# A graph network with a hand-drawn engine order: longer planned landing times for layer 0's turns and loads, the last h added up by VectorE and GpSimd, and x loaded ahead of adj

## The chip, the core and the metric

The kernel runs on one core of one Trainium2 chip. A core has five engines that take instructions in order, each from its own queue: TensorE (PE, matrix products into PSUM), VectorE (DVE), ScalarE (ACT), GpSimd (POOL) and SyncE (SP, which here issues nearly all DMAs). PEld in the profile is PE's loading of weights. Engines wait for each other through semaphores. The metric is the device time of one execution in microseconds (us); lower is better.

## What is computed

The input x is 32 batches of 512 nodes with 128 features; adj is one 512 x 512 matrix.

```python
# layer 0: seven terms; both adjacencies are adj
y = x W0 + (adj x)(W1 + W4) + (adj^2 x)(W2 + W5) + (adj^3 x)(W3 + W6)
h = layernorm(x + y)
h0 = h
for _ in range(5):                      # layer 1: gated steps
    m = adj h                           # in_matrix and out_matrix are both adj
    u = h u3.T + ub3
    z = sigmoid([m, m] w3.T + b3 + u)
    r = sigmoid([m, m] w4.T + b4 + u)
    hv = tanh([m, m] w5.T + b5 + (r h) u5.T + ub5)
    h = (1 - z) h + z hv
out = layernorm(h0 + h)
```

Everything is fp32.

## The kernel before

Batches go in 16 pairs (q = 0 to 15, b = 0 and 1). Each pair goes through layer 0 (`layer0`, L692), then five steps (`pair`, L1022, s = 0 to 4). Products of two batches are done by Strassen's scheme with seven block products instead of eight (`seven`, L384), whose sums of operands are made by POOL (`add`, L501) and whose results are taken from PSUM by ACT copies (L376) and VectorE additions (L380). From pair 2 on, two pairs share one quarter-block product with adj (`quad_product`, L556). PE computes the transposed adj, adj^2 and the sums of their blocks (T at L228, TT at L243) once at the start.

**What sets the order.** The kernel first describes every operation to a planner (`Plan`, L47): its engine, a cost in us, what it comes after, which buffers it takes and gives back, a key, and `late`, the time between the end of its cost and the moment at which its result counts as there. Then `run` (L75) plays the engines through: whenever an engine is free, it takes the ready operation with the lowest key whose buffers are free, and emits it. That order, fixed before the launch, is the order in each engine's queue. The chip keeps to it: an instruction that waits holds up all that stand behind it in its queue. `KEYS` (L24) gives each pair its base key, `TT_KEY` and `SQ_KEY` those of the start's sums and of the square of adj. The slots (L157) are the buffers; `two` and `inside` are counters without a tile, which limit how many block products and pairs are open at once in the plan.

**Turns.** Between a step and the next, h has to be transposed. `turn` (L336) does it without PE: VectorE transposes 32 x 32 blocks (L351), SP writes them to memory by four DMAs (L343, cost 1.76, late 1.8), and one more DMA fetches them (L349, cost 0.35, late 2.8). In layer 0, `turn_nodes` (L356) uses it for x and for h0 and ends with an ACT copy (L361) from the fetched raw tile (a `v` slot, five of them) into xT or hT. Only pairs 14 and 15 in their last two steps use PE's transpose instead (L1090 and L1093, `ON_PE`).

**The end of the last two pairs.** `gates` (L890) makes z, r and hv. In an ordinary step POOL adds (1-z)h and z hv at L954. In the last step of pairs 14 and 15 (`quick`) it hands two parts over: h becomes (1-z)h (VectorE, L945 for pair 14, L933 for pair 15) and z becomes z hv (L947, L927). PE then adds three things in PSUM by products with the identity: h0, the transposed h part and the transposed z part (`finish`, L994, matmuls at L1002; `last_finish`, L957, matmuls at L968, where everything is done in halves). `norm` (L295) takes statistics on VectorE (L304, L305), raises to -1/2 on POOL (L308 to L313) and applies on ACT (L321) or, for the very last batch, on VectorE (L317).

**The start.** SP issues in the order of the keys: first half of the first x, two quarters of adj, second half of x, two more quarters of adj (L208), the second x (L198, its first half), w0 (L251), the gate weights (L271, L279), then the rest of x. The second x is `x_in[1]` at L220.

Of the kernel before, what the change touches and what calls it, by code (L numbers as in the profile page):

```python
# [15 lines left out]
NK = 4  # L16
# [6 lines left out]
ON_PE = {14: 2, 15: 2}  # L23
KEYS = [-2.0, 20.0, 50.0, 68.0, 88.0, 124.0, 154.0, 168.0, 186.0, 214.0, 234.0, 272.0, 298.0, 330.0, 346.0, 362.0]  # L24
LONG = 19.0
TT_KEY = 39.0
SQ_KEY = 16.0
KEPT = 3
# [98 lines left out]
def gnn_resnorm_kernel(  # L127
# [26 lines left out]
    def tiles(tag, n, shape=(P, N), pool=work):  # L154
# [20 lines left out]
        v=tiles("v", 5),  # L175
        two=[None] * 4,
        inside=[None] * 16,
    )
# [17 lines left out]

    def load_x(q, b):
        nc.sync.dma_start(plan[f"xg{q}"][:, b], x[2 * q + b].rearrange("(p k) c -> p k c", k=NK))  # L198

    def loaded_x(q, key, late=2.9):  # L200

        take = [("xg", f"xg{q}")]
        first = plan("SP", 0.42, lambda: load_x(q, 0), take=take, key=key, late=late)
        return first, plan("SP", 0.42, lambda: load_x(q, 1), after=[first], key=key, late=late)

# [5 lines left out]
    def first_x():  # L211
        emit = lambda: load_x(0, 0)
        a = plan("SP", 0.42, emit, take=[("xg", "xg0")], key=-99.0, late=2.9)
        b = plan("SP", 0.42, lambda: load_x(0, 1), key=-91.0, late=4.0)
        return a, b
# [3 lines left out]
    at_in = [in11, in21, load_adj(0, 1, -90.0), load_adj(1, 1, -90.0)]  # L219
    x_in[1] = loaded_x(1, -80.0, 5.5)  # L220

# [41 lines left out]
    w0_ready = plan("DVE", 2.3, layer0_weights, after=[w0_in], give=[("UY", "w0")], key=-40.0)  # L263


    ready = []

    def gate_weight(src, name):
        halves = lambda: plan[name][:, : 2 * P].rearrange("p (h o) -> p h o", h=2)
        w = const.tile([P, P], F32, tag=name, name=name)  # L270
        emit = lambda: nc.sync.dma_start(halves(), src.rearrange("(h c) o -> c h o", c=P))  # L271
        got = plan("SP", 0.45, emit, take=[("z", name)], key=23.0, late=6.5)
        emit = lambda: nc.vector.tensor_tensor(w, halves()[:, 0, :], halves()[:, 1, :], ALU.add)
        ready.append(plan("DVE", 0.28, emit, after=[got], give=[("z", name)], key=26.0))
        return w

    def plain(src, name):
        t = const.tile(list(src.shape), F32, tag=name, name=name)
        ready.append(plan("SP", 0.45, lambda: nc.sync.dma_start(t, src), key=23.5, late=4.0))  # L279
        return t  # L280
# [54 lines left out]

    def turn(src_of, dst_of, name, after, key, take=(), give=()):  # L336

        def put():
            for g in range(NR):
                nc.sync.dma_start(  # L343
                    plan[f"d{name}"][:, :, g, :].rearrange("r l f -> l r f"),
                    plan[f"v{name}"][g * R : (g + 1) * R, :].rearrange("l (r f) -> l r f", r=NR),
                )

        def fetch():
            nc.sync.dma_start(dst_of(), plan[f"d{name}"].rearrange("r l g f -> (r l) (g f)"))  # L349

        blocks = lambda: nc.vector.transpose(plan[f"v{name}"], src_of())  # L351
        t = plan("DVE", 0.7, blocks, after=after, take=[("v", f"v{name}")], give=give, key=key)
        t = plan("SP", 1.76, put, after=[t], take=[("d", f"d{name}")], give=[("v", f"v{name}")], key=key, late=1.8)
        return plan("SP", 0.35, fetch, after=[t], give=[("d", f"d{name}")], take=take, key=key, late=2.8)

    def turn_nodes(src_of, dst, name, after, key):  # L356

        raw = f"w{name}"
        src = lambda: src_of().rearrange("p k (s d) -> p s k d", d=R)
        t = turn(src, lambda: plan[raw], name, after, key, take=[("v", raw)])  # L360
        emit = lambda: nc.scalar.copy(  # L361
            plan[dst].rearrange("p (k r l) -> p k r l", k=NK, r=NR),
            plan[raw].rearrange("p (r k l) -> p k r l", k=NK, r=NR),
        )
        return plan("ACT", 0.6, emit, after=[t], give=[("v", raw)], key=key)
# [326 lines left out]
    def layer0(q, key, entered):  # L692
# [23 lines left out]
        def t_block(b, g):  # L716
            if not quad:
                return plan[f"t{q}_{b}"][:, g * HN : (g + 1) * HN]
            return plan[Mn][:, 2 * g + (q - SINGLE) % 2, b * HN : (b + 1) * HN]

        x_turned = []
        for b in range(2):
# [166 lines left out]

    def gates(name, m, h, after, u_done, quick, key, ends_here=False):  # L890

# [26 lines left out]
        if ends_here:  # L918

            new = []  # L920
            for g in range(2):
                c = slice(g * HN, (g + 1) * HN)
                emit = lambda c=c: mm(ph, u5s, rh, False, True, c)
                p4 = plan("PE", 0.43, emit, after=[p3, r], key=key + 0.3 + 0.1 * g)
                emit = lambda c=c: nc.scalar.activation(plan[ph][:, c], plan[ph][:, c], AF.Tanh, bias=hv_b)
                t = plan("ACT", 0.43, emit, after=[p4], key=key + 0.3 + 0.1 * g)
                emit = lambda c=c: nc.vector.tensor_tensor(plan[z][:, c], plan[ph][:, c], plan[z][:, c], ALU.mult)  # L927
                new.append(plan("DVE", 0.42, emit, after=[t, zs], key=key + 0.3 + 0.1 * g))
            plan("-", 0.0, lambda: None, after=new, give=[("bank", ph), ("rh", rh)], key=key)
            rest = f"rest{name}"  # L930
            emit = lambda: nc.scalar.activation(plan[rest], plan[pz], AF.Sigmoid, scale=-1.0)
            k = plan("ACT", 0.59, emit, after=[pre_z, zs], take=[("uT", rest)], give=[("bank", pz)], key=key + 0.2)
            emit = lambda: nc.vector.tensor_tensor(plan[h], plan[rest], plan[h], ALU.mult)  # L933
            k = plan("DVE", 0.69, emit, after=[k, r], give=[("uT", rest)], key=key + 0.2)
            return [k, k], new
        emit = lambda: mm(ph, u5s, rh, False, True)
# [3 lines left out]
        if quick:  # L940
# [6 lines left out]
            emit = lambda: nc.vector.tensor_tensor(plan[z], plan[ph], plan[z], ALU.mult)  # L947
            return k, plan("DVE", 0.69, emit, after=[t, zs], give=[("bank", ph)], key=key + 0.8)

# [7 lines left out]
    def last_finish(q, b, name, h, parts, h0_of, after, key, done):  # L957

        z = f"z{name}"
        keep, new = parts  # L960
        banks = [f"bt{name}{g}" for g in range(2)]
        over = []
        for g in range(2):
# [14 lines left out]
            t = plan("PE", 0.22, emit, after=list(after), take=[("bank", banks[g])], key=key + 0.6)  # L978
            emit = lambda summed=summed: summed(lambda k: plan[h][:, chunk(k)], True, False, False)
            t = plan("PE", 0.22, emit, after=[t, keep[g]], key=key + 0.1)  # L980
            emit = lambda summed=summed: summed(lambda k: plan[z][:, chunk(k)], True, False, True)
            over.append([plan("PE", 0.22, emit, after=[t, new[g]], key=key)])
        y = lambda k: plan[banks[k // H]][:, chunk(k % H)]
        give = [("bank", bank) for bank in banks] + [("hT", h), ("z", z)]
        normed = norm(NK, f"1_{2 * q + b}", y, lambda k: h0_of(b)[:, k, :], over, give, key + 0.2, b == 1)
# [8 lines left out]
    def finish(q, b, name, h, parts, h0_of, after, key, done):  # L994

        bn, z = f"bt{name}", f"z{name}"
        y = lambda k: plan[bn][:, chunk(k)]
# [12 lines left out]

        keep, new = parts
        emit = lambda: summed(lambda k: h0_of(b)[:, k, :], False, True, False)
        t = plan("PE", 0.44, emit, after=list(after), take=[("bank", bn)], key=key)
        emit = lambda: summed(lambda k: plan[h][:, chunk(k)], True, False, False)
        t = plan("PE", 0.44, emit, after=[t, keep], give=[("hT", h)], key=key)
        emit = lambda: summed(lambda k: plan[z][:, chunk(k)], True, False, True)
        t = plan("PE", 0.44, emit, after=[t, new], give=[("z", z)], key=key)
        over = norm(NK, f"1_{2 * q + b}", y, lambda k: h0_of(b)[:, k, :], [t], [("bank", bn)], key + 10, q == NP - 1 and b == 1)
# [3 lines left out]
    def pair(q, key0):  # L1022
# [6 lines left out]
        for s in range(STEPS):  # L1029
# [23 lines left out]
            if last and q < NP - KEPT:  # L1053
                emit = lambda: nc.sync.dma_start(plan[f"h0{q}"], plan[f"hd{q}"])
                take, give = [("h0", f"h0{q}")], [("hd", f"hd{q}")]
                fetched = plan("SP", 0.45, emit, after=[spilt] + got[0], take=take, give=give, key=key + 5, late=3.0)
            if s > 0:
# [11 lines left out]
            for b in range(2):  # L1069
# [3 lines left out]
                ends_here = quick and q == NP - 1  # L1073
                d = gates(nm, f"m{nm}", h[b], got[b], u_done[b], quick, key + 10 + 0.05 * b, ends_here)
                if ends_here:
                    last_finish(q, b, nm, h[b], d, h0_of, read[b], key + 10.3 + 0.05 * b, done)
                    h_done.append(d[0] + d[1])
                    continue
                if quick:
                    finish(q, b, nm, h[b], d, h0_of, read[b], key + 15, done)  # L1080
                    h_done.append(list(d))
                    continue
# [90 lines left out]
```

## Time and profile before

| what | value |
|---|---|
| median of 3 runs (lowest, highest) | 1514.92 us (1513.14, 1515.15) |
| the profiled execution: time, span | 1513.85 us, 1512.1 us |
| mean granted TensorE clock | 0.998 |
| busy share PE, VectorE, POOL, ACT | 99%, 68%, 56%, 50% |
| DMA queue, share of 16 engines | 33.6% |
| first matmul, last matmul's end | 3.62 us, 1503.46 us |

The page and its views are read so. A row of a timeline has start, duration, engine, line, operation, output<-input, shape and count, and in brackets the idle time before it and what ended it. `xN` counts records; a fp32 matmul is two records, and a transpose by PE one. SPq is SP's issuing of a DMA; its landing is another time. A matmul's end is modelled, so short waits of PE show better in the distance of starts than in idle time. A row of waits has the engine and line that waited, the one waited for, us in total, times, and the longest.

The shapes that matter: PE's products of one step and one batch are five of 128x512 (L1036, L898), 0.859 us each, and its share of seven block products, each two matmuls of 128x256 (L515, 0.864 us for the two). An addition of 128x512 takes 682 ns on VectorE (L952) and 1272 ns on POOL (L954). The DMAs land, median from the issue, after 1.8 us (d<-v), 2.8 us (X<-d and v<-d), 3.0 us (x), 4.7 us (adj) and 3.8 us (hd<-h, the 512 KB spill of h0).

### The profile page before, as it was taken

Reading aid. Unit: us, or ns where it says so; the run is one execution under the profiler, and the core shown is the slowest. Engines: PE = TensorE matmul, PEld = TensorE weight load, DVE = VectorE, ACT = ScalarE, POOL = GpSimd, SP = SyncE. Lnnn points to the kernel's source line nnn. Section 1 sums busy time; section 2 is a strip of 40 time slices with the busy share of each in tenths; the row PEclk is TensorE's granted clock in tenths of the full one; section 3 lists DMA queues with packets and bytes.
Section 4 is the critical chain, followed back from the end, with each engine's and each line's share of the span. In section 5 each row is a group of like instructions: output and inputs, shape, how many; then the busy total and the mean of one; then the engine's idle time right before and its main releaser. Section 6 shows DMA issues by size and latency. Waiting matters only on the chain.

```text
span 1512.1 us, 21105 instructions
## 1 busy us (share of the span) xinstructions
PE 1494.5 (99%) x6594; PEld 1045.6 (69%) x6594; DVE 1025.3 (68%) x2125; ACT 750.3 (50%) x1584; POOL 839.5 (56%) x1201
## 2 busy tenths in 40 slices
PE   8999999999999999999999999999999999999997
PEld 7877767666666767676776766676776776566665
DVE  6567676577766676767677576777577675766565
ACT  3354444553644554555455454645445545545454
POOL 4755835573644864766367454557654653544442
PEclk9999999999999999999999999999999999999999
DMA  3224423253233433343343243433542322432210
GB/s 96 71 56 112 113 70 105 70 146 91 79 103 92 138 106 104 96 121 94 88 124 86 77 128 103 119 91 83 148 123 60 90 71 79 118 97 77 74 46 35
DMA packets 166176, 142.91 MB, mean 95 GB/s; under 512 B 18992, under 2 KB 128048, under 8 KB 166064
## 3 DMA queue, kind: packets, MB, share of 16 engines
q1 hardware_dynamic: 166064, 141.57, 33.6%
q8 instruction: 52, 0.85, 0.2%
q14 instruction: 60, 0.49, 0.1%
HBM read 71.76 MB, written 69.73 MB: 94 GB/s over the span
## 4 chain that ended last, share of the span: by engine, by line
PE 93%; DMA 3%; SPq 2%; DVE 1%; issue 0%; ACT 0%; POOL 0%; POOLq 0%; DVEq 0%; ACTq 0%
PE bank L898 35%; PE bank L515 31%; PE bank L1036 9%; PE bank L755 6%; PE bank L820 5%; PE bank L619 5%; SPq L343 1%; DMA v<-d 1%; DMA d<-v 1%; PE bank L451 1%; DVE v L351 0%; PE bank L293 0%; DMA X<-d 0%; PE bank L1002 0%; DMA xg<-in_x 0%
## 5 line engine op out<-in xcount | busy, mean ns | idle before, releaser
L954 POOL TENSOR_TENSOR hT<-z,hT 128x512 f32<-128x512 f32 x156 | 197.8, 1272 | 286.0 <-DVE z L952 268.1
L515 PE MATMUL bank<-T,S 128*128 128x256 f32 x1232 | 307.9, 380 | 2.9 <-ACT m L376 2.4
L515 PEld LDWEIGHTS bank<-T,S 128*128 128x128 f32 x1232 | 229.0, 190 | 81.5 <-ACT m L376 34.8
L376 ACT COPY m<-bank 128x256 f32<-128x256 f32 x320 | 119.0, 372 | 274.3 <-PE bank L515 272.8
L515 PE MATMUL bank<-at,S 128*128 128x256 f32 x824 | 211.4, 380 | 0.1
L380 DVE TENSOR_TENSOR m<-bank,m 128x256 f32<-128x256 f32 x240 | 100.6, 419 | 141.2 <-PE bank L515 90.1
L515 PEld LDWEIGHTS bank<-at,S 128*128 128x128 f32 x824 | 153.1, 190 | 56.7 <-issue 35.3
L950 DVE TENSOR_TENSOR bank<-bank,hT 128x512 f32<-128x512 f32 x156 | 108.2, 695 | 108.5 <-ACT bank L938 107.4
L898 PE MATMUL bank<-m,w4s 128*128 128x512 f32 x320 | 159.5, 593 | 0.0
L1036 PE MATMUL bank<-hT,u3s 128*128 128x512 f32 x320 | 159.3, 593 | 0.0
L898 PE MATMUL bank<-rh,u5s 128*128 128x512 f32 (+1 forms) x324 | 159.1, 587 | 0.0
L898 PE MATMUL bank<-m,w3s 128*128 128x512 f32 x320 | 156.8, 593 | 0.0
L898 PE MATMUL bank<-m,w5s 128*128 128x512 f32 x320 | 155.4, 593 | 0.0
L906 ACT ACTIVATE bank<-bank 128x512 f32<-128x512 f32 x160 | 93.3, 583 | 116.0 <-DVE bank L904 115.4
L904 DVE SCALAR_TENSOR_TENSOR bank<-bank,b4s,uT 128x512 f32<-128x512 f32 x160 | 119.8, 751 | 44.3 <-PE bank L898 42.2
L1041 ACT ACTIVATE uT<-bank,ub3s 128x512 f32<-128x512 f32 x160 | 109.6, 686 | 80.8 <-PE bank L1036 79.4
L938 ACT ACTIVATE bank<-bank,hv_b 128x512 f32<-128x512 f32 x158 | 104.3, 662 | 75.5 <-PE bank L898 73.8
L911 DVE SCALAR_TENSOR_TENSOR bank<-bank,b3s,uT 128x512 f32<-128x512 f32 x160 | 119.1, 751 | 11.1 <-PE bank L898 9.6
L913 ACT ACTIVATE z<-bank 128x512 f32<-128x512 f32 x160 | 95.0, 595 | 59.3 <-DVE bank L911 53.6
L351 DVE STREAM_TRANSPOSE v<-hT 128x512 f32<-128x512 f32 x152 | 105.8, 700 | 20.7 <-POOL hT L954 17.8
L907 DVE TENSOR_TENSOR rh<-bank,hT 128x512 f32<-128x512 f32 x160 | 108.0, 680 | 6.8 <-ACT bank L906 5.7
L952 DVE TENSOR_TENSOR z<-bank,z 128x512 f32<-128x512 f32 x156 | 105.5, 682 | 1.8
(183 smaller groups left out, 2447.5 us busy)
## 6 DMA issues: line engine op xcount, KB each, us to landing
d<-v SPq DMA_DIRECT2D x832, 64.0 KB, 1.8
X<-d SPq DMA_DIRECT2D x152, 256.0 KB, 2.8
v<-d SPq DMA_DIRECT2D x56, 256.0 KB, 2.8
xg<-in_x SPq DMA_DIRECT2D x32, 256.0 KB, 3.0
out<-h SPq DMA_DIRECT2D x30, 256.0 KB, 2.1
hd<-h SPq DMA_DIRECT2D x13, 512.0 KB, 3.8
h<-hd SPq DMA_DIRECT2D x13, 512.0 KB, 3.9
at<-in_adjT SPq DMA_DIRECT2D x4, 256.0 KB, 4.7
```

The costliest lines, as they stand in the source:

```text
L351: blocks = lambda: nc.vector.transpose(plan[f"v{name}"], src_of())
L376: return "ACT", COPY[cols], lambda src: nc.scalar.copy(dst(i, j), src)
L515: nc.tensor.matmul(dst, lhsT=left[:, k, :], rhs=right[:, k, :], start=(first and k == 0), stop=(last and k == H - 1), skip_group_check=True,)
L898: nc.tensor.matmul(plan[dst][:, c], lhsT=w, rhs=plan[src][:, c], start=first, stop=last, skip_group_check=True)
L904: emit = lambda: nc.vector.scalar_tensor_tensor(plan[pr], plan[pr], b4s, plan[uT], ALU.add, ALU.add)
L907: emit = lambda: nc.vector.tensor_tensor(plan[rh], plan[pr], plan[h], ALU.mult)
L911: emit = lambda: nc.vector.scalar_tensor_tensor(plan[pz], plan[pz], b3s, plan[uT], ALU.add, ALU.add)
L950: emit = lambda: nc.vector.tensor_tensor(plan[ph], plan[ph], plan[h], ALU.subtract)
L952: emit = lambda: nc.vector.tensor_tensor(plan[z], plan[ph], plan[z], ALU.mult)
L954: emit = lambda: nc.gpsimd.tensor_tensor(plan[h], plan[z], plan[h], ALU.add)
L1036: emit = lambda bn=bn, hb=h[b]: nc.tensor.matmul(plan[bn], lhsT=u3s, rhs=plan[hb], start=True, stop=True)
L1041: emit = lambda bn=bn, uT=uT: nc.scalar.activation(plan[uT], plan[bn], AF.Identity, bias=ub3s)
```

## The change

Planner constants: four base keys move later or earlier by up to 8, the sums TT come later, the square earlier, and five block products may be open instead of four. The plan's landing times: 5.0 instead of 2.8 for the fetch of a `turn_nodes`, 5.0 instead of 3.0 for the fetch of spilled h0, 4.5 instead of 2.9 for x, 5.0 instead of 6.5 for the three gate weights, which (with the other small weights) moreover may not start before 26 us of the plan. The first x's second half goes ahead of adj in SP's queue. The second x is issued by ACT once the first block of pair 0's first product is there. In `gates` the last step adds z hv to h: on POOL for pair 14 and for batch 1 of pair 15, on VectorE in halves for batch 0 of pair 15; pair 15's (1-z)h goes from VectorE to POOL. The two finishes lose their third sum.

```diff
-KEYS = [-2.0, 20.0, 50.0, 68.0, 88.0, 124.0, 154.0, 168.0, 186.0, 214.0, 234.0, 272.0, 298.0, 330.0, 346.0, 362.0]
+KEYS = [-2.0, 20.0, 50.0, 68.0, 92.0, 118.0, 154.0, 168.0, 186.0, 214.0, 234.0, 268.0, 294.0, 322.0, 346.0, 358.0]
-TT_KEY = 39.0
-SQ_KEY = 16.0
+TT_KEY = 45.0
+SQ_KEY = 10.0
...
-        two=[None] * 4,
-        inside=[None] * 16,
+        two=[None] * 5,
+        inside=[None] * 17,
...
-    def loaded_x(q, key, late=2.9):
+    def loaded_x(q, key):
...
+        first = plan("SP", 0.42, lambda: load_x(q, 0), take=take, key=key, late=4.5)
+        return first, plan("SP", 0.42, lambda: load_x(q, 1), after=[first], key=key, late=4.5)
+
+    def second_x(after):
+
+        emit = lambda b: load_x(1, b, nc.scalar)
+        after = after + [place]
+        first = plan("ACT", 0.45, lambda: emit(0), after=after, key=-60.0, late=3.2)
+        return first, plan("ACT", 0.45, lambda: emit(1), after=after, key=-60.0, late=3.2)
...
-        b = plan("SP", 0.42, lambda: load_x(0, 1), key=-91.0, late=4.0)
+        b = plan("SP", 0.42, lambda: load_x(0, 1), key=-98.0, late=3.4)
...
-    x_in[1] = loaded_x(1, -80.0, 5.5)
...
+    place = plan("-", 0.0, lambda: None, take=[("xg", "xg1")], key=-99.0)
+    later = plan("-", 0.0, lambda: None, key=-99.0, late=26.0)
...
-        got = plan("SP", 0.45, emit, take=[("z", name)], key=23.0, late=6.5)
+        got = plan("SP", 0.45, emit, after=[later], take=[("z", name)], key=23.0, late=5.0)
...
-        t = turn(src, lambda: plan[raw], name, after, key, take=[("v", raw)])
+        t = turn(src, lambda: plan[raw], name, after, key, take=[("v", raw)], late=5.0)
...
+        if q == 0:
+            x_in[1] = second_x([got[0][0]])
...
-            emit = lambda: nc.vector.tensor_tensor(plan[h], plan[rest], plan[h], ALU.mult)
-            k = plan("DVE", 0.69, emit, after=[k, r], give=[("uT", rest)], key=key + 0.2)
-            return [k, k], new
+            emit = lambda: nc.gpsimd.tensor_tensor(plan[h], plan[rest], plan[h], ALU.mult)
+            k = plan("POOL", 1.27, emit, after=[k, r], give=[("uT", rest)], key=key + 0.2)
+            over = []
+            for g, c in enumerate(cols):
+                engine, us, by = ("POOL", 0.73, nc.gpsimd) if ends_here == 2 else ("DVE", 0.42, nc.vector)
+                emit = lambda c=c, by=by: by.tensor_tensor(plan[h][:, c], plan[h][:, c], plan[z][:, c], ALU.add)
+                over.append(plan(engine, us, emit, after=[new[g], k], key=key + 0.3 + 0.1 * g))
...
-            return k, plan("DVE", 0.69, emit, after=[t, zs], give=[("bank", ph)], key=key + 0.8)
+            t = plan("DVE", 0.69, emit, after=[t, zs], give=[("bank", ph)], key=key + 0.8)
+            emit = lambda: nc.gpsimd.tensor_tensor(plan[h], plan[h], plan[z], ALU.add)
+            return plan("POOL", 1.27, emit, after=[t, k], give=[("z", z)], key=key + 0.8)
...
-            emit = lambda summed=summed: summed(lambda k: plan[h][:, chunk(k)], True, False, False)
-            t = plan("PE", 0.22, emit, after=[t, keep[g]], key=key + 0.1)
-            emit = lambda summed=summed: summed(lambda k: plan[z][:, chunk(k)], True, False, True)
-            over.append([plan("PE", 0.22, emit, after=[t, new[g]], key=key)])
+            emit = lambda summed=summed: summed(lambda k: plan[h][:, chunk(k)], True, False, True)
+            over.append([plan("PE", 0.22, emit, after=[t, parts[g]], key=key)])
...
-        t = plan("PE", 0.44, emit, after=[t, keep], give=[("hT", h)], key=key)
-        emit = lambda: summed(lambda k: plan[z][:, chunk(k)], True, False, True)
-        t = plan("PE", 0.44, emit, after=[t, new], give=[("z", z)], key=key)
+        t = plan("PE", 0.44, emit, after=[t, parts], give=[("hT", h)], key=key)
...
-                fetched = plan("SP", 0.45, emit, after=[spilt] + got[0], take=take, give=give, key=key + 5, late=3.0)
+                fetched = plan("SP", 0.45, emit, after=[spilt] + got[0], take=take, give=give, key=key + 5, late=5.0)
```

Since the order is drawn up anew from these numbers, nearly every row of every engine's queue stands elsewhere in the changed program; PE's operations are the same but for the 16 sums of z.

## The prediction

> **What bounds the kernel now.** I read the page first, for the busiest engine, then PE's waits, then ACT's waits, then the timeline round the longest PE wait, and last the timeline of the tail.
>
> ```profile
> PE 1494.5 (99%) x6594; PEld 1045.6 (69%) x6594; DVE 1025.3 (68%) x2125; ACT 750.3 (50%) x1584; POOL 839.5 (56%) x1201
> ...
> PE 93%; DMA 3%; SPq 2%; DVE 1%; issue 0%; ACT 0%; POOL 0%; POOLq 0%; DVEq 0%; ACTq 0%
> ```
>
> PE has 99% of the span, and the chain that ended last is 93% PE. Time can leave only as PE work, as PE waits, or at the two ends. PE's own waits are few (us in total, times, longest):
>
> ```profile
> PE bank L293 <- DMA xg<-in_x: 4.2, 2, 3.6
> PE bank L515 <- ACT m L376: 2.4, 2, 1.7
> PE bank L755 <- ACT UY L376: 1.1, 1, 1.1
> PE bank L515 <- ACT uT L376: 0.5, 1, 0.5
> PE bank L293 <- ACT h L321: 0.4, 1, 0.4
> PE bank L619 <- DVE M L377: 0.2, 1, 0.2
> ```
>
> Since the modelled end of a matmul hides short waits, I also took PE's start-to-start times against the cadence of undisturbed rows (two 256-column matmuls 0.864 us, one of 512 columns 0.859, one of 128 columns 0.223, a transpose 0.11). The excess: 2.3 us by 7.7 us (x and adj landing), 0.6 at 38.1, 2.5 from 51.0 to 56.2, and 4.1 after that: 0.3 at 65, 0.6 at 138, 1.86 at 187.5, 0.88 at 249.8, 0.16 at 216, 0.35 at 985.6. Some 9.5 us, with nothing between 986 and the tail. Before them lie 3.62 us to the first matmul, behind them a tail of 8.6 us from PE's end (1503.46) to 1512.1.
>
> ACT's waits say what lies behind the largest:
>
> ```profile
> ACT xT L361 <- DMA v<-d: 22.8, 17, 5.2
> ACT hT L361 <- DMA v<-d: 8.6, 9, 1.9
> ```
>
> L361 is the copy that ends a turn of layer 0's tiles through memory. The timeline of the longest wait, its lines picked out:
>
> ```profile
> 179.41 0.45 SPq L1049 DMA_DIRECT2D hd<-h  x1
> ...
> 179.90 0.43 SPq L349 DMA_DIRECT2D v<-d  x1
> ...
> 186.42 0.62 ACT L361 COPY xT<-v 128x512 f32<-128x512 f32 x1 [5.21 <-DMA v<-d]
> ...
> 186.94 0.36 ACT L376 COPY m<-bank 128x256 f32<-128x256 f32 x1
> ...
> 187.45 1.10 PE L515 MATMUL bank<-T,S 128*128 128x256 f32 x4 [1.69 <-ACT m L376]
> ```
>
> The fetch, issued just after a 512 KB store, took 6.5 us; the plan allows 2.8. ACT runs in order, so the copy at L376, whose bank was full, sat behind L361 and PE behind it. The waits at 249.8 (L361 idle 1.63 us) and 51.0 (L361 idle 2.17 us) have the same shape.
>
> **Part 1, the sum of h moved off PE.** For pairs 14 and 15, 16 matmuls by the identity (sums of z) go. L1002's groups of four start 0.89 us apart: 16 x 0.223 = 3.57 us of PE work. Pair 14's eight (1.79 us) are on the path. In their place pair 14 gets two POOL adds of 1.27 us (L954's row). By the built order some 6 us of PE rows stand between its last u5s product and the sums that need the adds; the way there is 0.2 + 0.66 (tanh) + 0.69 + 1.27 + hand-overs = 3.2 us, so it is covered; without the cover each batch would show 1.3 us.
>
> For pair 15 I count from the first w4s product (1491.22 is zero): last sum at +12.24, last statistic +14.5, end +20.88. The changed order has four h0 sums less behind zero (0.89 us, moved ahead of it) and eight z sums less, and PE would be done at +9.55 if nothing made it wait. But the built program makes the second u5s half of each bank wait for the tanh of its first half, and each z product wait for both halves. ACT has z of batch 1, a norm row and the 1-z sigmoid after all four tanhs. Step by step, rows of before: first u5s half ends +5.58, tanhs +5.78 to +6.67, second halves end +6.8 and +7.25, z product +7.0 to +7.43, its tanhs +7.5 to +8.4, then ACT 0.6 + 0.45 + 0.6 to +10.05, POOL's (1-z)h 1.27 to +11.4, two half adds of 0.73 (L502's row of that size) to +12.9, transposing sums to +13.45, two statistics to +14.5. That is the old +14.5, hence no more than 0.1 us for the end. What stays is that zero itself comes 1.79 - 0.89 = 0.89 us earlier. **Tail: -1.0 us** (bounds -2.0 and +0.8, by what ACT and POOL find in front).
>
> A rule speaks against this part. GPSIMD Engine Reference, 4.1, sends elementwise work to VectorE, GpSimd being about twice as slow with two inputs. The trace has L954 at 1272 ns and VectorE's same-size add (L952) at 682. By the rule batch 1's three steps on VectorE would take 0.69 + 0.42 + 0.42 = 1.53 us for POOL's 2.73, and the tail -2.2; the change keeps them on POOL, so the row's sum stands.
>
> **Part 2, longer landing times.** A fetch of a turn_nodes goes from 2.8 to 5.0 us in the plan, so ACT's order has 2.2 us more of other work ahead of each such copy. Of the 26 waits at L361 all but one (5.21) are 2.2 or less. The one would keep 3.0, and PE had 3.5 us of cover there (5.21 - 1.69). So 1.86 + 0.88 go: -2.74. The other 1.35 us after 57 us have other causes and I keep them; the new keys also redraw everything, and in the new order one quarter product follows its producer directly, +0.2 to +0.5. The raw tiles are held longer, out of five v slots; DVE's waits for one (L351 on d<-v) are 2.3 us in all, off PE's path. **After 57 us: -2.4** (bounds -3.9 and +1).
>
> **Part 3, the start.** Both halves of the first x go ahead of adj. The six loads are the same, and T's first sum waits for adj until 7.75 in before; a transfer behind that one doesn't come earlier. PE does its first four groups by about 7.1 instead of 8.57 but then waits for T. What is gained is DVE's time: T's sums took 1.23, 0.88 and 1.21 us beside POOL's sums of x, and 0.68 alone. SBUF — State Buffer, the section on the shared port pair ("The single rule"), says a VectorE instruction with two SBUF inputs and a GpSimd one that reads SBUF block each other. With x at about 4.4, POOL's sums are done before T's start: some 0.5 us by the first T product. With the rule unheeded the start would give 0; I take -0.5 (0 to -1.5). The second x moves from SP, where its second half was issued behind ten weight loads at 11.60, to ACT, two issues of 0.33 to 0.59 us (SP's rows) about 8.3; the next thing in ACT's queue, a copy of transposed adj, is due only about 10. It costs nothing; uncovered it would be 1.2. POOL's sums of it start near 12.0 instead of 14.5, which helps layer 0's sums behind them. At 38.1 one transpose now stands between producer and user: -0.3. At 51.0 the copy stands two ACT rows later: 1.3 + 0.5 go, but the normalised h0 that PE needs at 56.2 hangs on statistics, POOL's two powers (ready 53.6) and four ACT rows of 0.5, about 55.3: -0.9. The weights now go out on SP behind pair 2's x and the first turn's four writes (about 30 to 34 us); with 6.0 us, the longest row of such a load, they land by 38, and VectorE asks for them about 37.5. Below nothing they can't be, since they were early before; above, 1 us. I take +0.2. **Start: -1.5** (bounds -3.5 and +1).
>
> The slots "two" and "inside" are counters of the plan without a tile, the later spill fetch is only a plan time: nothing beyond the order.
>
> **Sum.** -1.0 - 2.4 - 1.5 = -4.9. The profiled execution took 1513.85 us (span 1512.1 and 1.75 around it): 1508.95. It lies 1.07 below the median of the runs, 1514.92; carried to the median, 1510.0. What is late next: PE itself, with 1485.7 us of work.
>
> **Rivals.** (a) The forecast, 1510.0; chance 0.60. (b) Most of what hides in waits goes: L361's and the others' too, and the start passes on its 1.5 us: -1.5 - 3.8 - 2.5 = -7.8, 1507.1. For it: from 986 us on before shows no wait at all. Against: the start's chain of norms. 0.18. (c) The redrawn order opens as many waits as it closes, and the change does not do what its landing times say: tail -1.0, start -0.9, nothing else: -1.9, 1513.0. For it: 6.5 us is longer than the 5.0 planned, and h and x turns share SP with all others, where SP waited 77 us for writes to land. 0.17. (d) Slower, by the turn of h between steps when only pairs 13 to 15 are left: PE rows between the last u5s of one step and the next product exceed the way over VectorE, POOL, SP and two landings by only 2.6 us at the closest place, near 1390. Each turn that takes over 2.6 us more than its rows costs the rest at once. To end slower it would have to lose 4.9 + 3 us, three turns at 5 us over. Against: the old order has the same 2.6 us there and no wait. 1518.5, chance 0.05.
>
> **Numbers.** A measurement of this kernel can tell 0.2% (3.0 us) from no change: faster is below 1511.9. (a) lies below it in nearly all of its width (0.55 of 0.60), (b) wholly, (c) above it, so faster 0.73, same 0.22, slower 0.05. The range 1506.5 to 1513.2 leaves out the outer end of (b), a part of (c), and (d).
>
> **What would show it.** L361's copies (new line L370) waiting under 10 us in all instead of 31.4, and no PE wait of over 1 us after 57 us: part 2. PE's matmul count 32 records lower, and the last statistic +14.5 behind the first w4s: part 1. T's sums at 0.7 us and the second x landed by 13 us: part 3. I am wrong if PE shows new waits on ACT or POOL between 60 and 1450 us of over 3 us, or if VectorE stands at the weights' sums.

## The result, and the profile after

The changed kernel takes 1511.80 us (median of 18 runs, 1510.82 to 1512.88), the kernel before 1515.04 beside it (18 runs, 1513.10 to 1516.82): ratio 0.998, 95% interval 0.9972 to 0.9987. That is 3.2 us less, where 4.9 were forecast. The profiled execution took 1512.07 us, its span 1510.3, which is 1.8 less than in the profile before; the clock was 0.997.

First the page's busy times and the shares of the chain that ended last:

```profile
PE 1493.2 (99%) x6562; PEld 1042.3 (69%) x6562; DVE 1024.4 (68%) x2125; ACT 750.7 (50%) x1584; POOL 848.7 (56%) x1207
...
PE 94%; DVE 2%; POOL 1%; issue 1%; DMA 1%; SPq 0%; ACT 0%; POOLq 0%; DVEq 0%
```

PE has 32 records less, the 16 sums of z, and the chain holds 94% of PE. DMA and SP's queue fell from 5% together to 1%, VectorE and POOL rose from 1% to 3%. Next PE's waits and ACT's waits at the copy of a turn (in total, times, longest; L370 is the old L361):

```profile
PE bank L302 <- DMA xg<-in_x: 3.7, 1, 3.7
PE bank L986 <- POOL hT L950: 2.2, 1, 2.2
PE bank L524 <- DMA at<-in_adjT: 1.0, 1, 1.0
PE bank L766 <- POOL S L511: 0.9, 2, 0.8
PE bank L524 <- ACT S L504: 0.6, 1, 0.6
```

```profile
ACT xT L370 <- DMA v<-d: 4.0, 4, 2.4
ACT hT L370 <- DMA v<-d: 2.4, 2, 2.0
```

L370 waits 6.4 us in 6 waits, where L361 waited 31.4 in 26, and PE waits for none of ACT's block copies (m) any more. In their place stand single waits for POOL and for adj. The one for POOL is in the last batch, whose (1-z)h and two half adds stand in a row:

```profile
1499.25 1.26 POOL L945 TENSOR_TENSOR hT<-uT,hT 128x512 f32<-128x512 f32 x1 [3.43 <-ACT uT L943]
...
1500.59 1.40 POOL L950 TENSOR_TENSOR hT<-hT,z 128x256 f32<-128x256 f32 x2
...
1501.37 1.90 PE L986 MATMUL bank<-ident,hT 128*128 128x128 f32 x8 [2.23 <-POOL hT L950]
```

The account, by PE's distances of starts less the cadence (as in the prediction; places above 0.15 us added up, read to some 0.2 us; the first column holds, besides waits, the slower cadence of PE's first matmuls, see below):

| kernel (profiled) | to 59 us | 59 to 1450 us | behind 1450 us |
|---|---|---|---|
| before | 5.4 | 4.1 | 0.0 |
| changed | 5.5 | 3.2 | 3.2 |

The last column's 3.2 lies inside the tail, which in spite of it has its old length: 20.8 us from the first product with w4s to the end, 20.9 before. So the span's 1.8 us are 0.9 of PE work ahead of the tail and 0.9 of waits in the middle. The start gave nothing. The medians say 1.5 us more than the two profiles, because the profiled execution before was a fast one: 1.2 us below its kernel's median, the changed kernel's 0.3 above (below, on the start).

### The profile page after: what moved, and what is told of

Its sections match the earlier page's. It is cut to its first block, busy times and chain, and to the rows that moved or that the text cites. A ratio compares the mean times of both kernels' runs of the same rounds, so it can differ in the third digit from the quotient of the medians.

```text
span 1510.3 us, 21064 instructions
## 1 busy us (share of the span) xinstructions
PE 1493.2 (99%) x6562; PEld 1042.3 (69%) x6562; DVE 1024.4 (68%) x2125; ACT 750.7 (50%) x1584; POOL 848.7 (56%) x1207
## 4 chain that ended last, share of the span: by engine, by line
PE 94%; DVE 2%; POOL 1%; issue 1%; DMA 1%; SPq 0%; ACT 0%; POOLq 0%; DVEq 0%
PE bank L909 35%; PE bank L524 32%; PE bank L1049 9%; PE bank L766 6%; PE bank L831 6%; PE bank L628 4%; PE bank L460 1%; PE bank L302 0%; POOL rstd L320 0%; POOL S L511 0%; DVE M L685 0%; DMA at<-in_adjT 0%; DVE UY L685 0%; PE bank L1018 0%; DMA X<-d 0%
```

## Experiments

My theory from the two profiles was this. A: the landing times do take L361's waits away; x ahead of adj costs PE 1.6 us at the start (first product with T at 10.74 us instead of 9.13), the redrawn order opens small waits, and POOL's adds stand on the path in the tail. The rivals stand with each run. Each was timed beside the kernel before, whose median there was 1514.85 to 1515.56 us. The last three columns are PE's excess as above, in us.

| run | us | ratio to before (95%) | to 59 | 59 to 1450 | behind |
|---|---|---|---|---|---|
| e1_adj_back | 1513.43 | 0.9995 (0.9987 to 1.0003) | 8.2 | 3.5 | 3.1 |
| e2_x_ahead | 1514.74 | 0.9999 (0.9991 to 1.0007) | 7.6 | 3.2 | 0.0 |
| e3_pe_sums | 1513.07 | 0.9986 (0.9979 to 0.9992) | 6.0 | 2.7 | 1.4 |
| e4_tail_dve | 1511.64 | 0.9980 (0.9973 to 0.9987) | 6.0 | 3.2 | 2.7 |
| e5_three_copies | 1512.12 | 0.9984 (0.9978 to 0.9991) | 4.3 | 2.5 | 0.0 |
| e6_after_late28 | 1521.24 | 1.0046 (1.0033 to 1.0059) | 4.9 | 13.0 | 3.1 |
| e7_before_late5 | 1511.37 | 0.9976 (0.9967 to 0.9984) | 6.2 | 0.65 | 0.0 |
| e8_both | 1513.36 | 0.9992 (0.9986 to 0.9999) | 7.6 | 2.6 | 2.6 |
| e9_late5_sums | 1510.97 | 0.9972 (0.9962 to 0.9982) | 6.7 | 0.3 | 2.9 |
| e10_old_keys | 1510.75 | 0.9973 (0.9963 to 0.9982) | 5.8 | 1.4 | 2.9 |
| e11_last_keys | 1510.19 | 0.9968 (0.9956 to 0.9980) | 5.2 | 2.4 | 3.1 |
| e12_last_keys_start | 1510.80 | 0.9969 (0.9958 to 0.9981) | 6.6 | 0.5 | 3.1 |

**The order of the first loads, alone and undone.** The first run gives SP the old order of issue in the changed kernel, the second gives the kernel before the new one. No other queue is touched.

```diff
+    b = x_in[0][1]; b.emit, in11.emit, in21.emit = in11.emit, in21.emit, b.emit
```
```diff
+    b = x_in[0][1]; in11.emit, in21.emit, b.emit = b.emit, in11.emit, in21.emit
```

> The changed kernel with one thing undone: the first x's second half and the first two quarters of adj go out on SP in the old order again (x, adj, adj, x, adj, adj); every other queue stands exactly as in the changed kernel. Theory A (x ahead of adj costs PE at the head, since PE's work on adj cannot begin before adj lands and PE is the bound from there on): first product with adj at about 4.5 instead of 6.64 us, first product with T at about 9.1 instead of 10.74, PE waits between 38 and 57 us no more than 0.6 us larger, so 1.0 to 1.6 us faster than the changed kernel, about 1510.5. Rival B (the head is covered by later waits; the gain of VectorE's lone sums of T is what counts): the same within 0.4 us or slower, and the sums of T beside POOL's take over 0.8 us again.

> The kernel before with one thing done: both halves of the first x ahead of adj on SP; every other queue stands exactly as in the kernel before. Theory A: first product with T 1.3 to 1.7 us later than in the kernel before (about 10.6 instead of 9.13), and the kernel 1.0 to 1.6 us slower, about 1516.3. Rival B (the prediction's step): first product with T 0.5 us earlier, time 0.5 us lower.

A fell. With the old order of loads the changed kernel is not faster but 1.6 us slower. The start of the timeline of that run (start, duration, engine, what it did; in brackets the idle time and what ended it):

```profile
2.13 0.47 SPq L198 DMA_DIRECT2D xg<-in_x  x1
...
3.69 1.09 PE L302 MATMUL bank<-ident,xg 128*128 128x128 f32 x4 [3.69 <-DMA xg<-in_x]
7.66 1.11 PE L302 MATMUL bank<-ident,xg 128*128 128x128 f32 x4 [2.88 <-DMA xg<-in_x]
8.44 1.20 DVE L234 TENSOR_TENSOR T<-at 128x512 f32<-128x512 f32 x1 [7.58 <-DMA at<-in_adjT]
8.56 3.62 PE L524 MATMUL bank<-at,xg 128*128 128x256 f32 x8
```

The new plan has both transposes of x first in PE's queue. When x's second half is issued fourth, behind two quarters of adj, it lands about 7.6 us, and the products with adj, which came at 6.64 in the changed kernel, stand behind that transpose until 8.56. The old PE queue has a product with adj between the two transposes and can use the old order of loads. The second run is the mirror image: PE waits 2.1 us for adj at 6.72 and reaches T at 11.41, yet the time is that of before within about 1.1 us, where A expected 1.0 to 1.6 more. PE's lag behind the profile before is 2.3 us at T, 1.9 at 58 us and 0.9 at 188: the wait for L361 there is 0.45 us instead of 1.86. A PE that comes later waits less for a late copy. So the order of loads and PE's queue belong together, and each alone loses at the start.

**Is the new start better than the old?** Five kernels have exactly before's queues for the first 40 us: before, e5_three_copies, e7_before_late5, e9_late5_sums and e12_last_keys_start. Their first product with T starts at 9.13, 8.95, 10.83, 11.40 and 11.33 us. The new start gives 9.74, 9.80, 10.72, 10.74 (the changed kernel), 10.95 and 11.18 in six. The waits to 59 us are 5.8 us in the mean of the five (4.3 to 6.7), 5.6 in the mean of the six (4.9 to 6.0). By these means the new start is worth 0.3 us, which five executions can't tell from nothing.

What made the start before look so good are PE's own rows, here of before and then of e7_before_late5, which has the same queues:

```profile
4.50 1.91 PE L515 MATMUL bank<-at,xg 128*128 128x256 f32 x4
6.99 0.88 PE L293 MATMUL bank<-ident,xg 128*128 128x128 f32 x4 [0.57 <-DMA xg<-in_x]
7.71 1.03 PE L515 MATMUL bank<-at,xg 128*128 128x256 f32 x4
9.13 1.10 PE L515 MATMUL bank<-T,S 128*128 128x256 f32 x4
```

```profile
7.36 1.12 PE L293 MATMUL bank<-ident,xg 128*128 128x128 f32 x4 [1.03 <-DMA xg<-in_x]
8.27 1.91 PE L515 MATMUL bank<-at,xg 128*128 128x256 f32 x4
10.83 1.37 PE L515 MATMUL bank<-T,S 128*128 128x256 f32 x4
```

In the second, x's second half comes only 0.4 us later, the product with T 1.7 us. The same four records, bank<-at,xg, take 1.91 us there and 1.03 in before: PE's first matmuls start twice as far apart (0.43 us for 256 columns, later 0.216), and the change to the shorter distance came at about 7.5 us in before and e5_three_copies, at 11.3 to 11.8 in the three others. Those two executions lie 1.2 and 1.5 us below the medians of their kernels, the three others within 0.2 us of theirs. So the 1.6 us between my two profiles were, for the most part, the luck of one execution. The new order had no such luck in any of the six: its eight products with adj come in one row, and at least seven of them ran at the longer distance (here the changed kernel):

```profile
6.64 3.78 PE L524 MATMUL bank<-at,xg 128*128 128x256 f32 x8 [1.02 <-DMA at<-in_adjT]
10.74 1.03 PE L524 MATMUL bank<-T,S 128*128 128x256 f32 x4
```

**The last h.** First z summed by PE again (the diff shows pair 14; pair 15's two places are done alike), the rest as changed; then the last batch's three steps on VectorE.

```diff
-            emit = lambda: nc.gpsimd.tensor_tensor(plan[h], plan[h], plan[z], ALU.add)
+            emit = lambda: None
-            return plan("POOL", 1.27, emit, after=[t, k], give=[("z", z)], key=key + 0.8)
+            return plan("POOL", 1.27, emit, after=[t, k], key=key + 0.8)
...
-        emit = lambda: summed(lambda k: plan[h][:, chunk(k)], True, False, True)
+        emit = lambda: (summed(lambda k: plan[h][:, chunk(k)], True, False, False), summed(lambda k: plan[f"z{name}"][:, chunk(k)], True, False, True))
```
```diff
-            emit = lambda: nc.gpsimd.tensor_tensor(plan[h], plan[rest], plan[h], ALU.mult)
+            emit = lambda: (nc.vector if ends_here == 2 else nc.gpsimd).tensor_tensor(plan[h], plan[rest], plan[h], ALU.mult)
-            k = plan("POOL", 1.27, emit, after=[k, r], give=[("uT", rest)], key=key + 0.2)
+            k = plan(*(("DVE", 0.69) if ends_here == 2 else ("POOL", 1.27)), emit, after=[k, r], give=[("uT", rest)], key=key + 0.2)
...
-                engine, us, by = ("POOL", 0.73, nc.gpsimd) if ends_here == 2 else ("DVE", 0.42, nc.vector)
+                engine, us, by = ("DVE", 0.42, nc.vector)
```

> The changed kernel with the adds of z times hv to h (POOL's for pair 14 and for batch 1 of pair 15, VectorE's halves for batch 0) left out and z transposed and added by PE again, 16 matmuls, at the same places in PE's queue; (1-z)h of pair 15 stays on POOL. Theory A (PE's work ahead of the tail counts fully, the two half adds on POOL cost in the tail about what they save): pair 14 costs 1.8 us again, the tail gets 0.5 to 0.9 us shorter since POOL's last two adds (1.4 us) are replaced by four or eight matmuls (0.45 to 0.9 us): 0.9 to 1.3 us slower than the changed kernel, about 1512.9. Rival C (pair 14's adds are not covered and cost PE a wait there): under 0.5 us slower.

> The changed kernel with the last batch's (1-z)h and its two half adds on VectorE instead of POOL, and on VectorE ahead of most of batch 0's statistics; PE, ACT and SP stand as in the changed kernel. Theory A (POOL's 1.26 + 1.40 us stand on the path to the last transposing sums): 0.68 + 0.75 us instead, the last sum and the end 1.2 us earlier, about 1510.6. Rival D (batch 0's statistics, now behind them on VectorE, or the powers on POOL set the end): under 0.4 us.

The first came out as A had it: 1.27 us slower, in its profile 1.8 us of PE work back ahead of the tail (between 983 us and the first w4s product), and the tail 0.6 us shorter, 20.2 us. The second is no faster than the changed kernel beyond the noise (0.16 us). Its steps were as short as the rows promised, but see VectorE's queue there, and POOL's at its end:

```profile
1499.26 0.61 ACT L943 ACTIVATE uT<-bank 128x512 f32<-128x512 f32 x1
1499.74 0.29 DVE L313 BATCH_NORM_STATS2 st<-bank 128x6 f32<-128x128 f32 x1
1500.06 0.18 DVE L314 BATCH_NORM_AGGREGATE mv<-st 128x2 f32<-128x6 f32 x1
1500.16 0.66 DVE L945 TENSOR_TENSOR hT<-uT,hT 128x512 f32<-128x512 f32 x1
1500.74 0.29 DVE L313 BATCH_NORM_STATS2 st<-bank 128x6 f32<-128x128 f32 x1
1501.06 0.18 DVE L314 BATCH_NORM_AGGREGATE mv<-st 128x2 f32<-128x6 f32 x1
1501.16 0.72 DVE L950 TENSOR_TENSOR hT<-hT,z 128x256 f32<-128x256 f32 x2
...
1504.13 0.18 DVE L314 BATCH_NORM_AGGREGATE mv<-st 128x2 f32<-128x6 f32 x1
1504.42 0.20 POOL L322 TENSOR_TENSOR shift<-shift,rstd 128x4 f32<-128x4 f32 x1
1504.71 0.23 POOL L317 TENSOR_SCALAR rstd<-mv 128x4 f32<-128x4 f32 x1
```

L945 takes 0.66 instead of 1.26 and the two halves of L950 0.72 instead of 1.40, but batch 0's statistics stand between, so that the last statistic ends 14.1 us behind the first w4s product instead of 14.75. Half of these 0.6 us goes at POOL's powers: still at those of batch 0, POOL begins the last ones 0.4 us after that statistic instead of 0.1. From the first w4s product to the end it is 20.5 us instead of 20.8. Rival D holds with both its reasons, and the rule of the Trainium skill that the prediction weighed (GPSIMD Engine Reference, 4.1) is right on the price and yet decides nothing here. Both ends together:

> The changed kernel with both the old issue order of the first x and adj on SP and the last batch's (1-z)h and half adds on VectorE. Theory A: the two gains lie at the two ends of the kernel and add up: 2.2 to 2.8 us faster than the changed kernel, about 1509.3. Rival: either of them is covered by something that only shows when both are made, the sum is under 1.5 us.

1513.36, that is e1_adj_back again (1513.43), whose edit it holds: the shorter steps on VectorE add nothing to it, and A, which expected 1509.3, fell.

**L361, alone.** Three copies moved back by two places in ACT's queue, in the kernel before, nothing else; the edit holds the copy's emission until two more of ACT's have gone out:

```diff
+    def step(self, op): self.behind = self.behind and (self.behind[0] - (op.engine == "ACT"), self.behind[1]); self.behind = self.behind if not self.behind or self.behind[0] else self.behind[1]()
...
-                    op.emit()
+                    op.emit(); self.step(op)
...
+            if name not in ("x2_1", "x5_0", "x6_0"): return copy(plan[dst], plan[raw])
+            plan.behind = (3, lambda d=plan[dst], r=plan[raw]: copy(d, r))
```

> The kernel before with three of ACT's copies L361 (those behind which PE stood at 51.0, 187.5 and 249.8 us) moved behind the two ACT instructions that follow them; all other queues stand exactly as before, and no landing time of the plan is changed. Theory A (the copy stood too early in ACT's queue, and a bank's copy stood behind it): PE's start-to-start excess at 187.5 (1.86 us) and 249.8 (0.88) goes and nothing of it comes back before 1450 us; at 51.0 most of 1.3 goes but part comes back by 57 us; the kernel 2.7 to 3.5 us faster than before, about 1512. Rival E (PE meets the next late producer instead): the excess after 57 us falls by under 1.5 us, the time by under 1.5 us.

A holds: 2.84 us less, with no landing time changed. ACT and PE at the place of the longest wait:

```profile
183.75 1.03 PE L515 MATMUL bank<-at,S 128*128 128x256 f32 x4
183.94 0.58 ACT L376 COPY UY<-bank 128x512 f32<-128x512 f32 x1 [0.52 <-PE bank L619]
184.61 1.89 PE L515 MATMUL bank<-T,S 128*128 128x256 f32 x8
185.41 0.62 ACT L361 COPY xT<-v 128x512 f32<-128x512 f32 x1 [0.88 <-DMA v<-d]
```

PE's two products with T,S, which stood 1.86 us apart beyond their cadence, are one row of eight, and ACT waits for the same fetch behind the block copies. The wait at 250 is gone too; at 65 and 138 some 0.6 and 0.5 us came in, as PE now is there earlier. ACT still waits 23.1 us at L361 in all: only the waits with a copy behind them for which PE stands count.

**The landing time, alone and undone.**

```diff
-        t = turn(src, lambda: plan[raw], name, after, key, take=[("v", raw)], late=5.0)
+        t = turn(src, lambda: plan[raw], name, after, key, take=[("v", raw)], late=2.8)
```
```diff
-        t = turn(src, lambda: plan[raw], name, after, key, take=[("v", raw)])
+        t = turn(src, lambda: plan[raw], name, after, key, take=[("v", raw)], late=5.0)
```

> The changed kernel with the landing time of a turn_nodes fetch in the plan back at 2.8 us; everything else as changed; the order of all queues is drawn up anew. Theory A (the landing time removes L361's waits, but they are only worth what PE loses behind them): waits of ACT at L370 rise from 6.4 us to 20 us or more, PE's excess after 57 us from about 3.2 to 4.5 to 6 us; 1 to 3 us slower, about 1514. Rival F (the landing time does nothing, the new keys did the rest): waits at L370 under 12 us and the time within 0.5 us.

> The kernel before with the landing time of a turn_nodes fetch in the plan at 5.0 instead of 2.8 us, and no other change; the order of all queues is drawn up anew. Theory A: waits of ACT at L361 fall from 31.4 us to under 12 us, the excess at 187.5 and 249.8 goes; without keys fitted to it the order may open others of up to 1.5 us: 1 to 2.7 us faster, about 1513. Rival F: the waits at L361 fall but the time stays within 0.5 us, as PE waits for others.

These two settle most. The landing time alone takes 3.6 us off the kernel before, more than A expected and as much as the whole change. The changed kernel without it takes 1521.24, 6.3 us more than before. PE's waits and ACT's at L361 in the kernel with the landing time alone:

```profile
PE bank L293 <- DMA xg<-in_x: 4.6, 2, 3.5
PE bank L755 <- POOL S L502: 0.7, 1, 0.7
PE bank L515 <- ACT S L495: 0.5, 1, 0.5
PE bank L515 <- ACT uT L376: 0.5, 1, 0.5
```

```profile
ACT xT L361 <- DMA v<-d: 3.1, 3, 1.4
ACT hT L361 <- DMA v<-d: 0.3, 1, 0.3
```

Behind 57 us PE loses only the 0.65 us at 139; of the 4.1 in the kernel before, 3.4 are gone. And without it, under the changed kernel's keys:

```profile
ACT xT L370 <- DMA v<-d: 27.9, 17, 5.0
ACT hT L370 <- DMA v<-d: 11.6, 9, 2.2
```

```profile
187.14 0.62 ACT L370 COPY xT<-v 128x512 f32<-128x512 f32 x1 [4.98 <-DMA v<-d]
187.66 0.36 ACT L385 COPY m<-bank 128x256 f32<-128x256 f32 x1
187.93 0.69 ACT L1054 ACTIVATE uT<-bank,ub3s 128x512 f32<-128x512 f32 x1
188.06 0.42 DVE L389 TENSOR_TENSOR m<-bank,m 128x256 f32<-128x256 f32 x1 [1.60 <-ACT m L385]
188.18 1.10 PE L524 MATMUL bank<-T,S 128*128 128x256 f32 x4 [1.50 <-ACT m L385]
```

It is the place and the pattern of before. Such waits recur at 66, 188 and 542 us (1.5 to 1.9 us each), and further ones for VectorE, ACT and POOL between 700 and 1060 bring the middle to 13 us, more than A expected. So the other parts of the change together bring no gain that shows (1511.80 with them, 1511.37 without), and in the middle they cost: 3.2 us of excess instead of 0.65. Which?

**Parts put together.** The first of the next two is before with the landing time (the diff above) and the change's own edits of the gates and of the two finishes; the second is the changed kernel with all keys and counters old.

```diff
-KEYS = [-2.0, 20.0, 50.0, 68.0, 92.0, 118.0, 154.0, 168.0, 186.0, 214.0, 234.0, 268.0, 294.0, 322.0, 346.0, 358.0]
+KEYS = [-2.0, 20.0, 50.0, 68.0, 88.0, 124.0, 154.0, 168.0, 186.0, 214.0, 234.0, 272.0, 298.0, 330.0, 346.0, 362.0]
...
-TT_KEY = 45.0
-SQ_KEY = 10.0
+TT_KEY = 39.0
+SQ_KEY = 16.0
...
-        two=[None] * 5,
-        inside=[None] * 17,
+        two=[None] * 4,
+        inside=[None] * 16,
```

> The kernel before with two parts of the change alone: the landing time of a turn_nodes fetch at 5.0 us in the plan, and the sum of h moved off PE (adds on POOL and VectorE, 16 matmuls fewer). Keys, the start and all other times of the plan as before. Theory G (the landing time alone makes the whole gain of the change; the sums give about 1 us; what the new keys, the new start and the other times bring is lost again in the middle): excess of PE between 57 us and the tail about 0.7 us, as with the landing time alone, PE's work ahead of the tail 0.9 to 1.8 us less, 1510.3 us (0.5 to 1.5 us below the landing time alone and below the changed kernel). Rival H (the tail gives the sums back, since the adds stand on the path there): within 0.4 us of the landing time alone, 1511.4.

> The changed kernel with the base keys, the two keys of the start and the two counters of open products and pairs back at their old values; the landing times, the start's loads and the sums as changed. Theory G (the new keys, drawn up for another order, open small waits between 57 us and the tail): excess there 1.5 us or less instead of 3.2, time about 1.5 us below the changed kernel, 1510.3. Rival I (the small waits come with the new start or the other landing times, not with the keys): excess 2.5 us or more there and 1511.5 or above.

With the old keys the changed kernel takes 1510.75, 1.05 us less than with the new ones, and its middle has 1.4 us of waits instead of 3.2. Theory G holds in direction, but the two intervals overlap. The sums bring 0.4 us to the landing time alone, near rival H and within the noise. Between the two runs of this pair lie only the start, its loads and the other landing times: 0.2 us. PE's rows ahead of the last gates, before with landing time and sums, show where they stay:

```profile
1484.49 1.13 PE L515 MATMUL bank<-T,S 128*128 128x256 f32 x4 [0.46 <-ACT m L376]
1486.09 1.13 PE L515 MATMUL bank<-T,X 128*128 128x256 f32 x4 [0.46 <-ACT m L376]
```

With the landing time alone the last pair's two products with u3s (at 1484.21 and 1485.93) stand one between each two of these and fill the time that ACT takes to empty the bank. Without pair 14's sums of z the planner has drawn those products ahead into the sums' places (1477.78 and 1481.25), and PE stands here instead: excess 0.63 and 0.74 us, for some 1.3 us of work saved ahead of the last gates (16 records of 0.112 us less, 4 of the h0 sums moved ahead). The work went, and waits of its size came. The last two runs put the new keys of the last pairs alone to the old early ones, in the second and in the first of these two kernels (the line is shown against the changed kernel):

```diff
-KEYS = [-2.0, 20.0, 50.0, 68.0, 88.0, 124.0, 154.0, 168.0, 186.0, 214.0, 234.0, 272.0, 298.0, 330.0, 346.0, 362.0]
+KEYS = [-2.0, 20.0, 50.0, 68.0, 88.0, 124.0, 154.0, 168.0, 186.0, 214.0, 234.0, 268.0, 294.0, 322.0, 346.0, 358.0]
```

> The changed kernel with the two keys of the start, the two counters and the base keys of pairs 4 and 5 at their old values, and those of pairs 11, 13, 14 (index from 0: 11, 12, 13) and 15 at the new ones. PE's order is that of the run with all old keys up to about 900 us and a new one behind. Theory J (the early keys cost the small waits between 57 and 800 us, the late ones spare the two waits of 0.63 and 0.74 us ahead of the last pair's gates): excess between 57 us and the last pair's first w4s product about 1.4 us instead of 2.8 (all old keys) or 3.2 (changed kernel); 1509.4 us. Rival K (the waits ahead of the last gates come whatever the keys, since PE lost the 16 matmuls that filled them): 1510.8, as with all old keys.

> The kernel before with the landing time of a turn_nodes fetch at 5.0, the sums of h moved off PE and the new base keys of pairs 11 to 13 and 15; the start, its loads and all other times as before. It differs from the other run of this call in the start alone (and what is redrawn for it). Theory L (the new start is worth nothing that can be seen): within 0.5 us of the other run, 1509.7; rival M (the prediction's 1.5 us for the start): 1.0 us or more slower than the other.

Both waits ahead of the last gates are gone in both runs, so the late keys were what spared them, as J has it. The middle of the first is 2.4 us and not 1.4: 0.7 of it came with the late keys, at 981 and 1189. At 1510.19 and 1510.80 they are the two lowest ratios, 0.9968 and 0.9969, but their intervals overlap that of the changed kernel: that they beat it by 1.0 to 1.6 us is likely, not shown. That they differ by 0.6 us speaks for neither L nor M outright; 0.3 us is what the profiles gave the start, 0.2 us the pair before.

## Why the prediction was right, and where it was not

The time, 1511.80, lies in the range, 1.8 us above the forecast; faster it is, by 0.21%. By its own steps:

- **Part 2, -2.4 us.** The mechanism is right, and its gain is as large as that of the whole change: L361's copies stood too early in ACT's queue. It shows by itself (e5, e7) and undone (e6). The step that was mis-sized is "the other 1.35 us after 57 us have other causes and I keep them", with "+0.2 to +0.5" for the redrawing. With the landing time alone only 0.65 us of the 4.1 stayed (-3.4). In the changed kernel 2.5 us of waits for POOL, VectorE and ACT came in, of 0.3 to 0.8 each, so that the profile has -0.9; 1.8 of them go with the old keys (e10). I had the sum between the two by luck rather than by size: an order drawn anew has waits of its own, and keys are one draw of many.
- **Part 1, -1.0 us.** Right in the changed order: the last statistic ends +14.75 behind the first w4s product (forecast +14.5), the tail keeps its length, zero comes earlier by the 0.9 us of PE work, and undoing it costs 1.27 us. Whether it is a property of the edit is open: under the old keys the medians with and without it lie 0.4 us apart, within their intervals, and in the profile the products drawn into the sums' places leave PE waits of 1.4 us.
- **The rule against this part.** The "tail -2.2" on VectorE, and the -1.2 that I expected at the start of the runs, were both wrong: 0.16 us in the time. The price of the steps was right; VectorE's own queue was left out, and POOL's powers behind it.
- **Part 3, -1.5 us.** Wrong, about 0. T's sums do take 0.68 to 0.69 us each, as the row and the rule said, and POOL's sums are done before. The step that failed is "PE does its first four groups by about 7.1"; they were done at 10.2. Between the end of the transposes (5.4 us) and 7.1 there is room for no wait, and for eight records at 0.216 us each. But PE waited for adj until 6.64, and the row of eight took 3.6 us at 0.43 us each. From there PE is the bound, not VectorE. The second x went out at 10.95, not at 8.3, and cost no wait of PE that shows. Two pairs of runs differ in the start and the other landing times alone (e9 and e10, e12 and e11): 0.2 and 0.6 us for the new start, within the noise. Waits at 38, 51 and 56 went (0.4, 1.3 and 0.7 us), one of 0.9 for POOL at 55.5 came in.
- **The base.** I read 9.13 us for the first product with T as the start before. The four other executions of the same queues gave 8.95 to 11.40. And of the 2.3 us by 7.7 us that I put down to x and adj landing, only 0.8 are waiting; the rest is PE's longer distance of starts.
- **Rivals.** (b), most of the waits gone, did not come: 3.2 us stayed in the middle. Of (c), "the redrawn order opens as many waits as it closes", most came true but for the landing times, which did what they say. (d), the late turns near 1390, did not show: no wait of PE between 984 and 1450 us.

## What to carry to other kernels

In an order fixed before the launch, the landing time of a transfer is a promise to every instruction behind the one that waits: plan it later than the median (here 5.0 us was much better than the median's 2.8; no other value was run, and single fetches took up to 6.5), and count only those waits behind which the bound engine's supplier is queued. When a change draws the whole order anew, run its parts alone, for one part can carry all, and others bring nothing that shows. A saving in the bound engine's work counts only where that work was not filling a wait, and the first microseconds are not to be read from one execution.

## What the runs showed of the hardware

The first six loads, issued at the same times to within 0.1 us by the same queue, let the first product with T start anywhere between 8.95 and 11.40 us in five executions (8.95 and 10.83 on one chip). Two things differ. One is x's second half: PE had to wait for it until 6.99, 7.36, 7.86 and 7.97 us in four of them, and had it by 6.87 in the fifth. The Trainium skill (DMA: Bandwidth & Descriptors, "Queues, rings and completion order") says that one DMA copy is split over up to 16 rings, one on each DMA engine; no row here shows which of them came late. The other, and the larger part, is the moment at which the distance of PE's starts halves: about 7.5 us in two executions and 11.3 to 11.8 in three (9.2 to 11.7 in the six with the new start). What sets this moment no run here shows; PE's waits alone don't order it, for in e6_after_late28 PE hardly waits between 3.70 us and the change at 9.3.

The copy's fetch at the longest wait landed 6.5, 5.5 and 6.4 us after its issue in three kernels (before, e5_three_copies, e6_after_late28), so even a bad case is not one number.
